# A scratch fill behind every second gather of adjacency rows

## The chip, the cores and the metric

The kernel runs on one core of a Trainium2 chip. The metric is the device time of one execution in microseconds, as the median of several runs. Beside the runs there is one execution taken by the hardware profiler; it is longer, and the lines of the profile belong to it alone.

The engines are named as in the profile: PE is TensorE (PEld its weight loads), DVE is VectorE, ACT is ScalarE, POOL is GpSimd, SP is SyncE. SP, ACT and POOL also issue the DMAs.

## The reference

Input are features `x` (2708 x 512), a sparse non-negative adjacency matrix `adj` (2708 x 2708, about 0.3% of it filled, densest in the first rows and columns, its diagonal filled) and small weights. Four graph layers follow one another, each with a residual and a layer norm:

```python
x = ln(x + L0(x, adj)); x = ln(x + L1(x, adj)); x = ln(x + L2(x, adj, adj)); x = ln(x + L3(x, adj))
L0: A = adj + I; d = 1/sqrt(rowsum(A)); (d[:,None] * A * d[None,:]) @ x @ W.T + b
L1: inc = adj + mask/norm(mask); (inc @ x) / rowsum(inc)        # mask = adj > 0
L2: sigmoid(gate_a * (softmax-like attention over the mask of adj) @ h + gate_b * (adj @ (x @ Wg) + bg))
L3: relu(adj @ (bin(x) @ sign(weight).T))
```

Every layer multiplies `adj` with rows of features. What the kernel saves is the zeros of `adj`.

## The kernel before, in words

The rows are cut into 22 blocks of 128 (the last has 20 rows). For each output block `b` the kernel doesn't multiply with all 22 column tiles of `adj`. It packs: it looks up which nodes are neighbours of any row of the block, lists them 128 at a time (`ROOM[b]` lists for block `b`, 9 for block 1 down to 1 for block 21), and gathers for each list two things: the rows of `adj_t` for these nodes, only the 128 columns of block `b` (tile `packed[b]`, written once and used by all layers), and in each layer the feature rows of these nodes (`gathered`, L582). A matmul of the two then stands for a whole column of tiles. Block 0 is dense and stays so; some blocks take a few tiles directly (`DIRECT`).

**The search** (L669 to L1264) makes the lists and the packed tiles, and prepares layer 0 beside it. The blocks arrive in the order 1, 2, ... 21, 0, one per turn (`turn`, L1180). A turn loads two half rows of `adj` for a later block through SP's queue (`load`, four half-row buffers), sums them on ACT (L765), marks the non-zeros on DVE (L828) and counts them on PE (L849); it also transposes and projects `x` (L1030, L1045), scales the product by the inverse root of the degree and stores it with a DMA from ACT's queue into `y_rows` in device memory (L1055). The blocks are searched in nine groups:

```python
GROUPS = ((1,), (2, 3), (4, 5), (6, 7, 8), (9, 10, 11), (12, 13, 14), (15, 16, 17), (18, 19, 20), (21,))
```

A few turns after the last block of a group has arrived, `list_nodes` (L966) computes on DVE the group's lists, `index_of` (L987) and `row_at` (L993), and appends one entry per list to `to_fetch`. At the end of each turn `fetch` (L1011) issues an indirect DMA from POOL for each entry: the adjacency gather of 128 rows of 128 fp32 (L1013). For the first six groups (`RESTED`) it issues behind each gather a fill of a scratch tile of 128 x 384 fp32 with zeros on POOL (L1018). Nothing reads the scratch tile. There are 107 adjacency gathers in all: 9, 15, 13, 17, 15, 13, 12, 12 and 1 by group, so 82 of them are followed by a fill.

[...] the search is written out by hand and held in that order (`in_order`, L591). POOL's queue in and behind the search is thus: set-up, the 107 adjacency gathers with the 82 fills, then the gathers of layer 0 from `y_rows`, and so on through the layers. Each gather carries one of eight completion semaphores in turn, and waits until the gather eight before it has landed. The first gather of a group waits for that group's `row_at`.

**Layer 0** (L1399) goes through the blocks in the order 0, 1, 21, 2, 3, ...: it gathers feature rows from `y_rows` (L584, ten buffers), multiplies them with the packed tiles (L1316), adds and normalises on DVE (L1424, L654), and stores the block into `x1_rows` (L1428). Layers 1 and 2 do the same from `x1_rows` and `x2_rows`, layer 3 from `xw_rows`. Between the blocks of layer 0 stand other steps, which also read the packed tiles (`count_positive`, L1103).

Of the kernel before, what the change touches and what calls it, by code (L numbers as in the profile page):

```python
# [495 lines left out]
def sparse_layers(ctx, tc, x, adj, adj_t, w0_t, b0, w_sa, a_sa, w_gcnb, b_gcnb, wa, ba, wb, bb, w3_t,  # L496
# [22 lines left out]
    def direct(b: int):  # L519

        return tuple(range(NB)) if b == 0 else DIRECT.get(b, ())
# [147 lines left out]
    with tc.tile_pool(name="s_pre", bufs=1) as pre:  # L669
# [134 lines left out]
        group_of = {b: g for g in GROUPS for b in g}  # L804
# [201 lines left out]

        to_fetch = []
        RESTED = GROUPS[:-3]
        rest = pre.tile([P, 384], F32, name="s_rest")

        def fetch(n: int):  # L1011
            for b, t, row in to_fetch[:n]:
                nc.gpsimd.indirect_dma_start(  # L1013
                    out=packed[b][:, t + len(direct(b)), :], out_offset=None, in_=adj_t,
                    in_offset=bass.IndirectOffsetOnAxis(ap=row, axis=0), element_offset=b * P,
                )
                if group_of[b] in RESTED:
                    nc.gpsimd.memset(rest, 0.0)  # L1018
            del to_fetch[:n]

# [159 lines left out]
        def turn(at: int):  # L1180
# [46 lines left out]
            if found_in == SOON:  # L1227
                list_nodes(SOON)
            fetch(len(to_fetch))
            if at == NTURN:  # L1230
                count_block0()
# [824 lines left out]
def kernel(  # L2056
# [25 lines left out]
    flag = ctx.enter_context(tc.tile_pool(name="flag", bufs=1))  # L2082
    over = flag.tile([1, 1], I32, name="over")
    sparse_layers(tc, *args, over)
    n_over = nc.values_load(over[0:1, 0:1], min_val=0, max_val=-(-x.shape[0] // P))
    with tc.If(n_over > 0):
# [43 lines left out]
```

## Time and profile before

| | before |
|---|---|
| median of 3 runs | 1017.79 us (1017.23 to 1019.32) |
| profiled execution | 1063.61 us |
| its span, first to last instruction | 1061.9 us |
| mean granted clock of PE | 0.942 |
| busy in the span: PE, DVE, ACT, POOL | 893.4, 663.5, 385.5, 569.7 us |
| adjacency gathers, L1013 | 107, 115.8 us, first start 24.9, last start 208.8 us |
| scratch fills, L1018 | 82, 44.0 us, first start 26.5, last start 175.9 us |
| gathers from `y_rows`, L584 | 107, first start 210.0, last start 365.9 us |

Times in views of the profile count from the start of the span. A group of instructions is named by its line, engine, operation and tile; a wait names the instruction that waited and what released it. The busy time of a DMA on POOL is the time in which POOL issues it, not the transfer. "Remote" or "an unknown queue" as a releaser means that the profile does not show what ended the wait. A line number of the changed kernel is two higher behind the change (L1013 becomes L1014, L1018 becomes L1020).

### The profile page before, as it was taken

The page shows a single profiled execution, that of the slowest core. Times are in us where ns is not written, and L with a number is a line of the kernel's source. Part 1 is how long each engine was busy: PE and PEld are TensorE (multiplying, and loading weights), DVE is VectorE, ACT ScalarE, POOL GpSimd, SP SyncE. Part 2 cuts the span into 40 slices and gives each one's busy share as a digit, 9 for nine tenths or more (in the row PEclk, how much of TensorE's full clock was granted, in tenths as well). Part 3 has the DMA queues.
Part 4 walks back from the last instruction along what each step waited for, and adds up shares of the span by engine and source line. Part 5 has one row for each costly group of instructions (what it writes and reads, how often), then busy time and mean ns, then how long its engine had stood idle before and what let it go on. Part 6 is the DMA issues. An engine that isn't in the chain of part 4 may idle for free.

```text
span 1061.9 us, 13166 instructions
## 1 busy us (share of the span) xinstructions
PE 893.4 (84%) x3793; PEld 465.5 (44%) x3793; DVE 663.5 (62%) x2571; ACT 385.5 (36%) x821; POOL 569.7 (54%) x621
## 2 busy tenths in 40 slices
PE   1989996078788978899999999998889999689994
PEld 1545552022123324455455543443535555467772
DVE  4899998125566745345555346666758877646666
ACT  3566662000000013445344334333334333255554
POOL 1799998766666544555434034534434333057762
PEclk9899999589898988999999999999999999989996
DMA  9999984356776745666645266668677665299986
GB/s 265 349 321 322 336 263 144 82 171 209 231 210 207 227 139 145 184 209 189 208 144 168 95 233 216 238 223 288 205 230 230 200 195 201 80 269 311 321 233 214
DMA packets 96294, 231.16 MB, mean 218 GB/s; under 512 B 14204, under 2 KB 27884, under 8 KB 96212
## 3 DMA queue, kind: packets, MB, share of 16 engines
q0 software_dynamic: 46896, 139.22, 44.3%
q1 hardware_dynamic: 37368, 76.25, 20.9%
q10 hardware_dynamic: 11948, 14.76, 4.3%
q8 instruction: 32, 0.52, 0.2%
q14 instruction: 50, 0.41, 0.1%
HBM read 188.51 MB, written 31.71 MB: 207 GB/s over the span
## 4 chain that ended last, share of the span: by engine, by line
PE 52%; DVE 12%; DMA 11%; POOL 10%; another core or an unknown queue 6%; issue 6%; ACT 3%; ACTq 0%; POOLq 0%; SPq 0%; DVEq 0%
PE l L1316 14%; DMA xg<-x_rows,i 8%; PE h L1533 7%; POOL a L1013 6%; PE l L1999 4%; PE a L1744 4%; PE e L1744 4%; PE l L2038 3%; POOL s_rest L1018 3%; PE pg L1796 2%; PE pc L1796 2%; PE l L1371 2%; PE e L1566 1%; PE px L1857 1%
## 5 line engine op out<-in xcount | busy, mean ns | idle before, releaser
L1721 POOL DMA_INDIRECT xg<-x_rows,i x107 | 106.2, 993 | 170.3 <-PE a L1744 40.9
L584 POOL DMA_INDIRECT xg<-x_rows,i x107 | 103.6, 968 | 115.9 <-PE l L1316 73.1
L1013 POOL DMA_INDIRECT a<-in_adj_t_dram,row_at x107 | 115.8, 1082 | 46.6 <-DVE deg L773 21.4
L584 POOL DMA_INDIRECT xg<-y_rows,i x107 | 104.6, 978 | 52.6 <-issue 24.1
L1316 PE MATMUL l<-xg,a 128*64 128x512 f32 (+1 forms) x214 | 98.0, 652 | 27.5 <-DMA xg<-y_rows,i 26.9
L584 POOL DMA_INDIRECT xg<-xw_rows,i x76 | 79.6, 1048 | 38.6 <-issue 17.9
L1744 PE MATMUL a<-xg,a 128*64 128x512 f32 (+1 forms) x214 | 92.8, 603 | 4.5 <-DMA xg<-x_rows,i 4.5
L1744 PE MATMUL e<-xg,ae 128*64 128x512 f32 (+1 forms) x214 | 90.3, 603 | 2.7 <-ACT ae L1494 2.6
L1533 PE MATMUL h<-s_wsa,xt 128*128 128x256 f32 (+3 forms) x352 | 83.8, 392 | 6.9 <-ACT xt L1528 6.8
L1045 PE MATMUL y<-s_w,xt 128*128 128x512 f32 (+1 forms) x176 | 86.9, 640 | 0.0
L1316 PE MATMUL l<-xg,inc 128*64 128x512 f32 (+1 forms) x214 | 79.4, 613 | 3.6 <-DMA xg<-x_rows,i 3.1
L1533 PEld LDWEIGHTS h<-s_wsa,xt 128*128 128x128 f32 (+1 forms) x352 | 65.0, 189 | 33.5 <-ACT xt L1528 15.6
L1489 ACT ACTIVATE ae<-sl,xg 128x64 f32<-128x64 f32 (+1 forms) x107 | 37.5, 359 | 99.1 <-DMA xg<-x_rows,i 88.6
L765 ACT ACTIVATE unused<-arow 128x1408 uint8<-128x1408 f32 (+3 forms) x44 | 58.3, 1325 | 3.8 <-DMA x_rows<-s_zero 3.0
L1316 PEld LDWEIGHTS l<-xg,a 128*64 128x64 f32 (+1 forms) x214 | 25.1, 160 | 78.4 <-DMA xg<-y_rows,i 41.5
L1424 DVE SCALAR_TENSOR_TENSOR t<-l,s_dinv,f 128x512 f32<-128x512 f32 (+1 forms) x21 | 15.6, 744 | 64.6 <-remote 44.7
L1999 PE MATMUL l<-ws,pw 128*128 128x512 f32 (+1 forms) x210 | 51.5, 400 | 3.9 <-DVE pw L1927 3.9
L613 ACT ACTIVATE rsqs<-mv 128x1 f32<-128x1 f32 (+2 forms) x56 | 11.3, 202 | 112.1 <-DVE mv L642 45.8
L1540 DVE COPY h<-h 128x260 f32<-128x260 f32 (+1 forms) x20 | 8.6, 428 | 66.3 <-PE h L1533 47.5
L1045 PEld LDWEIGHTS y<-s_w,xt 128*128 128x128 f32 (+1 forms) x176 | 33.8, 203 | 36.5 <-issue 36.4
L1490 DVE SCALAR_TENSOR_TENSOR ae<-ae 128x128 f32<-128x128 f32 (+5 forms) x56 | 19.2, 343 | 45.8 <-ACT ae L1489 45.1
L1796 PE MATMUL pg<-s_wg,pt 128*128 128x256 f32 (+1 forms) x176 | 44.7, 392 | 2.8 <-ACT pt L1784 2.8
(302 smaller groups left out, 1887.2 us busy)
## 6 DMA issues: line engine op xcount, KB each, us to landing
arow<-in_adj_dram SPq DMA_DIRECT2D x21, 704.0 KB
arow<-in_adj_dram SPq DMA_DIRECT2D x21, 650.0 KB
x_rows<-f SPq DMA_DIRECT2D x41, 256.0 KB
aw<-in_adj_t_dram SPq DMA_DIRECT2D x21, 320.0 KB
f<-in_x_dram SPq DMA_DIRECT2D x20, 256.0 KB
y_rows<-yt ACTq DMA_DIRECT2D x20, 256.0 KB
out_dram<-f SPq DMA_DIRECT2D x20, 256.0 KB
x_rows<-h SPq DMA_DIRECT2D x19, 257.0 KB
```

What stands on the lines that cost most here:

```text
L584: nc.gpsimd.indirect_dma_start(out=t, out_offset=None, in_=src[:, :], in_offset=bass.IndirectOffsetOnAxis(ap=index[b][:, i : i + 1], axis=0),)
L765: nc.scalar.activation(unused[:m, : ar.shape[1]], ar, AF.Copy, accum_out=row_sums[:m, b, h : h + 1])
L1013: nc.gpsimd.indirect_dma_start(out=packed[b][:, t + len(direct(b)), :], out_offset=None, in_=adj_t, in_offset=bass.IndirectOffsetOnAxis(ap ...
L1018: nc.gpsimd.memset(rest, 0.0)
L1045: nc.tensor.matmul(ps[:m], xt[:, k, :m], w0[:, k, :], start=(k == 0), stop=(k == KC - 1))
L1316: nc.tensor.matmul(ps[r0:r1], weights, moving, start=(i == order[0]), stop=all(span(b, j) != (r0, r1) for j in order[order.index(i) + 1 :] ...
L1489: nc.scalar.activation(ev[:, i, :], sl, AF.Identity, bias=score)
L1533: nc.tensor.matmul(ps, xt[:, k, :m], w[:, k, :], start=(k == 0), stop=(k == KC - 1))
L1721: nc.gpsimd.indirect_dma_start(out=g, out_offset=None, in_=x2_rows[:, :], in_offset=bass.IndirectOffsetOnAxis(ap=index[b][:, t : t + 1], a ...
L1744: nc.tensor.matmul(ps[r0:r1], weights, moving, start=(i == order[0]), stop=all(span(b, k) != (r0, r1) for k in order[order.index(i) + 1 :] ...
L1796: nc.tensor.matmul(ps, pt[:, k, :m], w[:, k, :], start=(k == 0), stop=(k == KC - 1))
L1999: nc.tensor.matmul(whole[b], p[:r, h, b * P : (b + 1) * P], g[:r, :], start=(j == 0 and h == 0), stop=(j == NB - 1 and h == 1),)
```

## The change

The fill stands behind every second gather instead of behind each one. The counter counts all adjacency gathers, in the order in which they are issued; the fill follows the even ones of the first six groups.

```diff
         to_fetch = []
         RESTED = GROUPS[:-3]
+        fetched = [0]
         rest = pre.tile([P, 384], F32, name="s_rest")
 
         def fetch(n: int):
             for b, t, row in to_fetch[:n]:
                 nc.gpsimd.indirect_dma_start(
                     out=packed[b][:, t + len(direct(b)), :], out_offset=None, in_=adj_t,
                     in_offset=bass.IndirectOffsetOnAxis(ap=row, axis=0), element_offset=b * P,
                 )
-                if group_of[b] in RESTED:
+                fetched[0] += 1
+                if group_of[b] in RESTED and fetched[0] % 2 == 0:
                     nc.gpsimd.memset(rest, 0.0)
             del to_fetch[:n]
```

## The prediction

> **What bounds the kernel now.** I read the page first: its busy shares, its forty slices and its chain of waits. GpSimd (POOL) is busy in 54% of the span, TensorE (PE) in 84%, yet two POOL lines of the search stand in the chain.
>
> ```profile
> PE 52%; DVE 12%; DMA 11%; POOL 10%; another core or an unknown queue 6%; issue 6%; ACT 3%; ACTq 0%; POOLq 0%; SPq 0%; DVEq 0%
> PE l L1316 14%; DMA xg<-x_rows,i 8%; PE h L1533 7%; POOL a L1013 6%; PE l L1999 4%; PE a L1744 4%; PE e L1744 4%; PE l L2038 3%; POOL s_rest L1018 3%; PE pg L1796 2%; PE pc L1796 2%; PE l L1371 2%; PE e L1566 1%; PE px L1857 1%
> ```
>
> So the scratch fill itself (L1018) is 3% of the chain and the adjacency gathers (L1013) 6%. Next, the waits up to 270 us, and the busy time by stretch, to see who stands still while POOL works:
>
> ```profile
> DVE t L1424 <- remote: 41.5, 1, 41.5
> PE l L1316 <- DMA xg<-y_rows,i: 26.9, 5, 24.9
> ...
> 178.00:210.00 32.00, 2.92 (x14) 0.84 (x13) 10.27 (x36) 0.41 (x2) 24.65 (x24) 0.54 0.48 132
> ```
>
> The columns of the last line are the stretch, its length, and busy us of PE, PE's weight loads, DVE, ACT and POOL, then clock, DMA share and GB/s. From 178 to 210 us PE works 2.9 us, ACT 0.4, POOL 24.7 of 32: TensorE waits 24.9 us in one piece for the first gathered row tile of layer 0 (`xg<-y_rows`). Why is that gather late? The POOL timeline at three places (start, length, what, and after it the idle time before it):
>
> ```profile
> 144.47 1.00 POOL L1013 DMA_INDIRECT a<-in_adj_t_dram,row_at  x1 [0.16 <-issue]
> 145.47 0.47 POOL L1018 MEMSET s_rest<- 128x384 f32 x1
> 146.10 1.16 POOL L1013 DMA_INDIRECT a<-in_adj_t_dram,row_at  x1 [0.16 <-issue]
> 147.26 1.07 POOL L1018 MEMSET s_rest<- 128x384 f32 x1
> 148.49 1.34 POOL L1013 DMA_INDIRECT a<-in_adj_t_dram,row_at  x1 [0.16 <-issue]
> ...
> 207.51 0.94 POOL L1013 DMA_INDIRECT a<-in_adj_t_dram,row_at  x1 [0.30 <-issue]
> 208.76 0.94 POOL L1013 DMA_INDIRECT a<-in_adj_t_dram,row_at  x1 [0.30 <-issue]
> 210.01 0.94 POOL L584 DMA_INDIRECT xg<-y_rows,i  x1 [0.30 <-issue]
> ```
>
> From 45.57 to 226 us POOL has no pause longer than 0.31 us. Its queue holds 107 adjacency gathers, then the gathers of `y_rows`, in that order; the first of these starts at 210.01 because the last adjacency gather starts at 208.76. What it needs was there long before: the last store of `y_rows` is issued at 175.78, and SP's own read of `y_rows`, which waits for it, is issued at 177.97. So for 32 us only POOL's backlog holds layer 0 back. The search is not the limit there: its lists (`row_at` on DVE) start at 45.12, 69.30, 91.52, 111.52, 132.25, 151.97, 169.84 and 175.90, while POOL reaches the first gather of each of these groups at 45.57, 74.39, 98.27, 127.74, 155.56, 176.52, 193.78 and 208.76. Its lateness grows from 0.3 to 33 us.
>
> [...] the instruction takes 0.94 us, and by the packets the data land some 5 us after its start in the crowded search and 2.2 us near 205 us. [...] gathers of 0.94 us stretch to 1.4 to 1.6 while DVE is over 95% busy, and 13 of the 82 fills take about 1 us, not 0.44. [...]
>
> **The change, part by part.** On PE, DVE, ACT and SP the instructions and their order stay the same; only POOL's list changes. Of 82 fills (9+15+13+17+15+13 gathers of the first six groups) every odd one goes: 41.
>
> One removed fill: its own time, plus the 0.16 us that the next gather waits behind it, minus the 0.30 us between two gathers with nothing between (as from 178 us on). With the usual 0.44 us that is 0.44 + 0.16 − 0.30 = 0.30 us. With the mean over all fills (44.0 us / 82 = 0.537) it is 0.40.
>
> The first group's five (at 26.5, 30.2, 33.9, 37.1 and 40.2 us) are worth nothing: after its ninth gather POOL waits 4.9 us for the next list at 45.1, and only that wait grows. If that list came earlier, they would be worth another 1.5 us. There remain 36. Low end: 36 × 0.30 = 10.9 us. High end: the 36 that go took 19.6 us together, six of them long ones of about 1.04; 19.6 + 36 × (0.16 − 0.30) = 14.5 us. The 3.6 us between the ends [...] (6 × 0.6), which the next gather may inherit, since DVE is as busy as before. I take half of it: 12.7 us.
>
> Do lists then hold POOL up? By the third group POOL is 7 × 0.35 = 2.5 us ahead of before: 71.9, and the list is done at 70.0. By the fourth it is 14 × 0.35 = 4.9 ahead: 93.4 against 91.7. Behind that the gap widens: 118 against 112, 164 against 152. So no wait, by 1.7 us at the closest. Each gather also waits for the landing of the gather eight before it; eight new intervals are 8 × 1.6 = 13 us, against some 5 us to landing. No wait either.
>
> Gathers run earlier, beside the row loads. In 45.5 to 150 us the DMA engines are 94% busy at 315 GB/s. About six more gathers fall into it (57 with intervals of 1.86 us, 63 with 1.68). A gather costs 0.29 us of all sixteen engines (192 to 208 us: the software queue 25.4% of 16 us for 14 gathers). So 6 × 0.29 = 1.7 us later at most for the loads, hidden: between POOL's new first `y_rows` gather (210.0 − 12.7 = 197.3) and the ready `y_rows` (178) lie 19 us. If that cover went, the 1.7 us would count.
>
> From 197 us on everything stands in the same order behind POOL's gathers and PE's matmuls with them. DVE and ACT have finished their opening work of layer 0 at 190.2 us and wait for the first block, so nothing else is late next. In layer 0 POOL is busy 105 of 168 us and PE 136 by turns, each waiting for the other; both start 12.7 us earlier, and I carry it one to one through layers 1 to 3, which have no clock time of their own to wait for.
>
> Sum: span 1061.9 − 12.7 = 1049.2 us; the execution adds 1.7 around it (1063.6). The median of the runs, 1017.79, is 4.3% below the profiled execution, whose page cannot say where. POOL's chain leads by tens of us in the trace, so it should lead there too, and I take the same absolute gain: 1017.8 − 12.7 = 1005.1 us. Scaling it would change 0.5 us.
>
> **The rivals.**
>
> *Lists or loads eat part.* POOL speeds up, DVE's lists come a few us later by contention, and at the fourth group, whose margin is 1.7 us, POOL waits. For it: DVE is 99.3 of 104.5 us busy in the search, DMA 94%. Against it: that wait comes before 22 of the 36 fills that go, and these still gain afterwards: 22 × 0.35 = 7.7. Time about 1010 to 1014.
>
> *Nothing moves.* [...] a gather behind a gather stretches by what the fill took. For it: gathers of 1.4 to 1.6 us stand in the search only. Against it: the median gather there is 0.97, near the 0.94 without any DVE work, and most fills sit at 0.44[...]. Time 1017.8.
>
> *Slower: pairs of gathers hold DVE.* [...] `s_dia_pos` (L1095) takes 0.69 us at 114.30 and ends with POOL's gather; on one column it takes 0.13 at 159.07, so DVE pays for POOL. If each of 41 pairs cost DVE one gather more, 41 × 0.94 = 38 us, `y_rows` would be ready at 216 instead of 178, POOL's first gather of it would slip from 210 to 216: about 1024. It decides from 32/41 = 0.78 us per pair. Against it: POOL was never free before either (busy 95 of 104 us), and the share of time in which it executes falls[...].
>
> **How the numbers follow.** Gain as worked out 0.72, part of it 0.10, nothing 0.08, slower 0.10. Differences below about 0.2% (2 us) are what a measurement here cannot tell from no change: the three runs spread by 2.1 us. Faster 0.72 + 0.10 = 0.82, same 0.08, slower 0.10. The likeliest case alone: 1003.3 to 1006.9 by its two ends, 1001 to 1008 with the spread and with TensorE's clock, whose half-speed stretches may fall elsewhere. For eight in ten the second case comes in, and the edge of the third: 1001 to 1016.
>
> **What would show it.** Right: 41 fills of `s_rest`; first `y_rows` gather near 197; DVE's wait of 41.5 us at L1424 near 29; the last `row_at` still within 2 us of 175.9; gathers of the search at the same mean of about 1.1 us. Step wrong, lists: an idle POOL before L1014 for a DVE `row_at`. Step wrong, [...] longer gathers and a gain under 10 us at the first `y_rows` gather. Step wrong, carrying: that gather at 197 but the end not 12 us earlier. The whole is wrong if the search's last list moves beyond 195 us, because then DVE or the loads, not POOL's queue, set when layer 0 begins.

## The result, and the profile after

The changed kernel takes 1003.52 us (median of 6 runs, 1000.5 to 1007.23), the kernel before in the same comparison 1018.76 (6 runs, 1017.23 to 1022.14): a ratio of 0.9849, interval 0.9821 to 0.9876. That is 15.2 us less; 12.7 had been forecast, and 1003.52 lies inside the likeliest case's own range.

The kernel before itself took about 1017 us in some of the comparisons and about 1066 us in others (the 1017 level and the 1066 level below), so each comparison has its own runs of the kernel before beside it. The profile of before shown above (1063.61 us) is of the 1066 level, that of the changed kernel (1000.5 us) of the 1017 level. It was therefore not the profiler that made the profiled execution of before longer than its runs. To compare like with like there is a profile of the kernel before at the 1017 level as well (1022.25 us, span 1020.5; "the third run of before" below).

The page of the changed kernel, chain of waits:

```profile
PE 53%; DMA 20%; DVE 16%; issue 4%; ACT 3%; POOL 3%; ACTq 0%; POOLq 0%; DVEq 0%; SPq 0%
PE l L1318 11%; DMA xg<-x_rows,i 10%; PE h L1535 8%; DMA xg<-y_rows,i 7%; PE l L2001 5%; PE a L1746 4%; PE e L1746 4%; PE l L2040 3%; PE y L1047 3%; PE pg L1798 2%; DVE s_mask L828 2%; PE pc L1798 2%; PE e L1568 2%; PE a L1569 2%; POOL xg L584 1%
```

POOL's share of the chain is 3%; the scratch fill and the adjacency gather are no longer among the lines that the page names, and a line of the search on DVE (`s_mask`, L828) has come in. The same page of the third run of before:

```profile
PE 54%; DMA 19%; POOL 12%; DVE 8%; issue 4%; ACT 2%; ACTq 0%; POOLq 0%; SPq 0%
```

Here POOL has 12%. This shift alone shows little: in the first comparison below another profile of the kernel before has POOL at 2% and DVE at 15%, and POOL's queue still ends 27 us behind the last list in the changed kernel (194.44 and 167.48). The queue itself is the better witness. Next the waits up to 270 us and the stretch from 178 to 210 us (columns as in the prediction) of the changed kernel:

```profile
DVE t L1426 <- PE l L1318: 41.1, 7, 29.2
PE l L1318 <- DMA xg<-y_rows,i: 24.8, 12, 18.9
...
178.00:210.00 32.00, 12.80 (x29) 3.53 (x29) 4.06 (x20) 0.00 (x0) 24.38 (x26) 0.60 0.50 131
```

PE does 12.8 us of work in the stretch in which it did 2.9; its longest wait for the first gathered tile is 18.9 us instead of 24.9 (23.4 in the third run of before). POOL's timeline:

```profile
97.58 0.95 POOL L1014 DMA_INDIRECT a<-in_adj_t_dram,row_at  x1 [0.30 <-issue]
98.52 0.44 POOL L1020 MEMSET s_rest<- 128x384 f32 x1
99.12 1.56 POOL L1014 DMA_INDIRECT a<-in_adj_t_dram,row_at  x1 [0.16 <-issue]
100.98 0.99 POOL L1014 DMA_INDIRECT a<-in_adj_t_dram,row_at  x1 [0.30 <-issue]
...
162.10 0.44 POOL L1020 MEMSET s_rest<- 128x384 f32 x1
...
194.44 0.95 POOL L1014 DMA_INDIRECT a<-in_adj_t_dram,row_at  x1 [0.30 <-issue]
195.70 0.95 POOL L584 DMA_INDIRECT xg<-y_rows,i  x1 [0.30 <-issue]
```

Two gathers, one fill, with the 0.30 and 0.16 us between them that the forecast used; the first gather of `y_rows` at 195.70 (forecast 197.3). In the third run of before the queue ends so:

```profile
208.42 0.95 POOL L1013 DMA_INDIRECT a<-in_adj_t_dram,row_at  x1 [0.30 <-issue]
209.67 0.95 POOL L584 DMA_INDIRECT xg<-y_rows,i  x1 [0.31 <-issue]
```

Like for like, then, that gather moves by 209.67 − 195.70 = 14.0 us, and the median by 15.2.

### The profile page after: what moved, and what is told of

It is laid out like the page before. It is cut to its first block, busy times and chain, and to the rows that moved or that the text cites. A ratio compares the mean times of both kernels' runs of the same rounds, so it can differ in the third digit from the quotient of the medians.

```text
span 998.8 us, 13107 instructions
## 1 busy us (share of the span) xinstructions
PE 875.6 (88%) x3775; PEld 458.8 (46%) x3793; DVE 657.8 (66%) x2571; ACT 386.5 (39%) x821; POOL 549.6 (55%) x580
## 4 chain that ended last, share of the span: by engine, by line
PE 53%; DMA 20%; DVE 16%; issue 4%; ACT 3%; POOL 3%; ACTq 0%; POOLq 0%; DVEq 0%; SPq 0%
PE l L1318 11%; DMA xg<-x_rows,i 10%; PE h L1535 8%; DMA xg<-y_rows,i 7%; PE l L2001 5%; PE a L1746 4%; PE e L1746 4%; PE l L2040 3%; PE y L1047 3%; PE pg L1798 2%; DVE s_mask L828 2%; PE pc L1798 2%; PE e L1568 2%; PE a L1569 2%; POOL xg L584 1%
## 5 line engine op out<-in xcount | busy, mean ns | idle before, releaser
L1014 POOL DMA_INDIRECT a<-in_adj_t_dram,row_at x107 | 115.9, 1083 | 52.2 <-issue 24.9
L1047 PE MATMUL y<-s_w,xt 128*128 128x512 f32 (+1 forms) x176 | 83.6, 620 | 0.0
L638 DVE BATCH_NORM_STATS2 st<-t 128x6 f32<-128x512 f32 (+1 forms) x66 | 45.2, 685 | 0.2
```

The lines of the kernel that those rows point to most:

```text
L638: nc.vector.bn_stats(st[:m], t[:m])
L1014: nc.gpsimd.indirect_dma_start(out=packed[b][:, t + len(direct(b)), :], out_offset=None, in_=adj_t, in_offset=bass.IndirectOffsetOnAxis(ap ...
L1047: nc.tensor.matmul(ps[:m], xt[:, k, :m], w0[:, k, :], start=(k == 0), stop=(k == KC - 1))
```

## The experiments

Nothing reads the scratch tile, so every kernel here computes all that the reference does; only POOL's time and its place differ. All edits are given against the kernel before or against the changed one, as named.

The theory (the backlog): POOL's queue is the gate to layer 0, and the time is set by how much work stands in it ahead of the first `y_rows` gather, not by where fills stand. The rival (crowding): gathers close behind each other cost something elsewhere, so fewer fills lose again what they save.

### First: no fills, the same fills in pairs, the saved time put back at the end

The kernel before again:

> The kernel before, unchanged, profiled once more. In its first profile the last list (row_at) started at 175.9 us, in the changed kernel at 167.5. If fewer fills make DVE's search faster, it is again near 176 here. If the first profile was merely a slow execution (clock 0.942, 1063.6 us), it is near 168, the span near 1017, and the first gather from y_rows still near 207 to 210, since POOL's own instructions set that.

1068.61 us, ratio 1.0002 (0.9978 to 1.0026). This comparison fell on the 1066 level. The last list starts at 178.31 us and the first `y_rows` gather at 209.29, so the list is near 176 again and not near 168.

No fills at all:

```diff
-        RESTED = GROUPS[:-3]
+        RESTED = ()
```

> All 82 fills are gone. POOL's queue as the limit: 41 more fills of about 0.35 us leave, so the first gather from y_rows comes up to 14 us before 195.7, until POOL catches up with the lists; the last two groups still have 13 gathers of 1.25 us behind the list of 161 us, so not before 178: 178 to 185 us, and the kernel takes about 988 to 994 us. Lists as the limit: POOL idles before gathers of the fourth group onward and the gain is under 8 us. Pairs holding DVE: the lists come later than in the changed kernel by 5 us or more and the time is no better than 1003.

1102.33 us, ratio 1.0308 (1.0235 to 1.0380): slower. First `y_rows` gather at 239.6, against 209.3 in the kernel before beside it. So at this level crowding is real. The waits from 45 to 180 us say where it bites:

```profile
POOL a L1014 <- DVE s_own L1064: 42.9, 4, 14.1
ACT xt L1039 <- remote: 39.1, 4, 12.1
DVE s_dia_own L858 <- remote: 27.7, 4, 9.5
```

POOL now waits for lists, 42.9 us in four pieces, and DVE and ACT stand still for up to 12 us with no releaser shown. One of those stalls in the timeline of the same kernel:

```profile
86.32 0.64 PE L1032 MATMUL pt<-s_ident,f 128*128 128x128 f32 x4
...
92.17 0.94 POOL L1014 DMA_INDIRECT a<-in_adj_t_dram,row_at  x1 [0.30 <-issue]
93.42 0.94 POOL L1014 DMA_INDIRECT a<-in_adj_t_dram,row_at  x1 [0.30 <-issue]
96.48 0.16 DVE L858 SCALAR_TENSOR_TENSOR s_dia_own<-find,s_dia 128x1 f32<-128x1 f32 x1 [9.51 <-remote]
96.53 0.59 ACT L1039 COPY xt<-pt 128x512 f32<-128x512 f32 x1 [10.08 <-remote]
```

ACT's copy takes the four transposes that the record has ended at 86.96, but starts at 96.53; DVE resumes with it, about 3 us after the start of the last gather of the burst. That gather ends at 94.36 and POOL is idle from there to the end of the stall. No view prints it, but the trace also keeps when each semaphore was updated. DVE and ACT both wait here for the semaphore that PE updates, and its two updates stand at 96.45 and 96.51 us, 10.0 and 9.6 us after the end of the matmuls that send them (86.46 and 86.96). So the signal of PE came late; DVE and ACT took it within 0.03 us. By stretch (columns as in the prediction):

```profile
84.00:92.00 8.00, 6.76 (x44) 3.68 (x43) 2.90 (x14) 2.42 (x4) 6.04 (x7) 1.00 0.80 260
92.00:96.40 4.40, 0.00 (x0) 0.00 (x0) 0.00 (x0) 0.00 (x0) 1.89 (x2) 0.79 0.39 113
96.40:98.50 2.10, 0.85 (x13) 0.57 (x12) 1.73 (x9) 1.56 (x4) 0.00 (x0) 0.50 0.00 0
98.50:112.00 13.50, 11.47 (x87) 6.42 (x85) 10.88 (x47) 7.39 (x13) 2.96 (x3) 0.64 0.85 287
```

In 4.4 us nothing works but POOL's last two gathers, and PE's clock is at half after it: PE's last matmul before the stall ends at 91.25, and the granted clock is at 0.50 from 94.55 to 108.20. So to the 4.4 us without work comes a stretch of 13.65 us at half clock that began in the stall. What lowered the clock, and why PE's signal comes so late, the trace does not show.

Two fills behind every second gather, so that gathers stand in pairs but no fill is saved (against the changed kernel):

```diff
                 if group_of[b] in RESTED and fetched[0] % 2 == 0:
                     nc.gpsimd.memset(rest, 0.0)
+                    nc.gpsimd.memset(rest, 0.0)
```

> The gathers stay in pairs as in the changed kernel, but two fills stand behind each pair, so there are 82 again. POOL's queue as the limit: POOL's time is that of the kernel before within 2 us, first gather from y_rows at 207 to 211, and the kernel takes 1014 to 1020 us, as before. Pairing itself as the cause of the gain [...]: it stays near 1003.

1078.11 us, ratio 1.0113 (1.0050 to 1.0176); first `y_rows` gather 217.5, 8.2 us later than before. POOL's timeline:

```profile
123.98 0.95 POOL L1014 DMA_INDIRECT a<-in_adj_t_dram,row_at  x1 [0.15 <-issue]
125.24 0.94 POOL L1014 DMA_INDIRECT a<-in_adj_t_dram,row_at  x1 [0.31 <-issue]
126.18 0.44 POOL L1020 MEMSET s_rest<- 128x384 f32 x1
126.67 0.42 POOL L1021 MEMSET s_rest<- 128x384 f32 x1
127.25 1.05 POOL L1014 DMA_INDIRECT a<-in_adj_t_dram,row_at  x1 [0.16 <-issue]
```

A pair takes 3.27 us; two gathers each with its fill take 2 × (0.94 + 0.44 + 0.16) = 3.08. The 0.19 us are 0.30 instead of 0.16 between the gathers and 0.05 between the fills; for the 36.5 pairs from the second group on, 7 of the 8.2 us. The rest is the second group's list, which came 1.5 us later (46.12, not 44.64). The last list, at 179.83, is within 2 us of the kernel before beside it (178.31). So with two fills behind each pair the search is hardly delayed even at this level, although ACT waits there five times for PE without a seen releaser (15.4 us, 4.2 at most): the loss is mostly POOL's queue.

The changed kernel, with 36 fills put between the last adjacency gather and the first `y_rows` gather:

```diff
                 if group_of[b] in RESTED and fetched[0] % 2 == 0:
                     nc.gpsimd.memset(rest, 0.0)
+                if b == NB - 1:
+                    for _ in range(36):
+                        nc.gpsimd.memset(rest, 0.0)
```

> The changed kernel with 36 fills put back in one place, between the last adjacency gather and the first gather from y_rows. POOL's queue as the limit: 36 x 0.44 = 16 us later at that gather, at about 211, and the kernel takes 1003.5 + 16 = about 1019 us. If the gain came from the search (faster lists, DVE or loads freed from the fills), the search is as in the changed kernel, and the time stays under 1008.

1085.38 us, ratio 1.0183 (1.0118 to 1.0247); `y_rows` at 231.7. Its last adjacency gather starts at 212.0, 4 us later than in the kernel before beside it (208.0), although 41 fewer fills stand ahead of it. So at this level the search ate the saving. Whether the changed kernel alone still gains there was not in this comparison; it came in the last one.

### Second: the changed kernel again, the saving without pairs, a part of the change

This comparison fell on the 1017 level. The changed kernel:

> The changed kernel, unchanged, once more. Queue theory (POOL's queue alone decides, gathers in a row cost nothing): 0.982 to 0.988 of the kernel before wherever it runs, first gather from y_rows 13 to 15 us before that of the kernel before. Crowding theory (gathers in a row hold up TensorE's handing on of results while the search loads): where the kernel before takes about 1068 us, the search shows waits of ACT and DVE for TensorE that end with no seen releaser, the last list comes 5 us or more later than before, and the ratio is 0.995 or more; where it takes about 1018, none of this and 0.985.

1004.13 us against 1017.01, ratio 0.9863 (0.9807 to 0.9920); `y_rows` at 197.4.

A fill behind each gather, as before, but of half the width:

```diff
                 if group_of[b] in RESTED:
-                    nc.gpsimd.memset(rest, 0.0)
+                    nc.gpsimd.memset(rest[:, :192], 0.0)
```

> A fill behind every gather, as in the kernel before, but of 192 columns instead of 384. By the lengths of fills of 1, 128 and 384 columns (0.10, 0.20, 0.44 us) a fill of 192 takes 0.26 us, so POOL saves 0.175 us on each of 73 fills that count: 12.8 us, as much as the change. Queue theory: the same ratio as the changed kernel within 0.004. Crowding theory, where the kernel before takes about 1068 us: no two gathers stand in a row, so better than the changed kernel by 0.005 or more.

Ratio 0.9876 (0.9821 to 0.9932), median 1007.79; `y_rows` at 197.1. The median fill takes 0.278 us, 0.16 less than 0.44: over the 73 fills from the second group on 11.7 us, about as much as the change saves, and POOL starts on the second group 1.4 us earlier. The gain and the place of the first `y_rows` gather are those of the change, within the intervals. What counts at this level is POOL's time, not whether gathers stand in pairs.

All fills of the sixth group taken out, the others as before:

```diff
-        RESTED = GROUPS[:-3]
+        RESTED = GROUPS[:-4]
```

> The kernel before without the 13 fills of the sixth rested group alone (blocks 12 to 14), whose gathers ran from 155.6 to 175.9 us, when the row loads of the search had ended. Both theories: 13 x 0.30 to 0.40 = 4 to 5 us less, ratio 0.995 to 0.996, with the first gather from y_rows that much earlier and no new waits, since nothing is left to be crowded.

1013.24 us, ratio 0.9958 (0.9939 to 0.9978): 4.3 us of 1017.01. `y_rows` at 205.6, 4.0 us earlier than in the third run of before. Thirteen fills × 0.35 = 4.6. The last list, at 174.05, moved by only 1.7 us, and the queue ends 30 us behind it, so a faster search is not where this gain comes from.

The kernel before, for its profile at this level:

> The kernel before, unchanged, as the profile to compare these three with: first gather from y_rows at 207 to 210 us and the last list at 175 to 179 where it takes about 1068 us; where it takes about 1018, by the queue theory the same gather near 209, and the last list near 168.

1022.25 us in this one run; first `y_rows` gather at 209.67. No wait with an unknown releaser stands in its search, nor in that of the changed kernel at this level.

### Third: no fills at the 1017 level

> All 82 fills gone, once more. If the loss of 3% seen where the kernel before took 1068 us is a matter of gathers in a row and nothing else, it is slower here too, wherever it runs, with waits for TensorE without a seen releaser in the search. If it needs the conditions of those runs, then, with the kernel before at about 1017 us, the queue theory holds to the end: first gather from y_rows at 178 to 187 us and about 0.970 to 0.978 of the kernel before.

> The changed kernel on the same chip as the run without fills. With the kernel before at about 1017 us: 0.984 to 0.988 again. With it at about 1068 us: crowding theory 0.995 or more, queue theory 0.982 to 0.988.

Without any fill (the edit of the first comparison): 991.95 us against 1017.60, ratio 0.9736 (0.9698 to 0.9774). The changed kernel in the same comparison: 1002.21, 0.9857 (0.9799 to 0.9914). The end of POOL's search queue without fills:

```profile
182.51 0.95 POOL L1014 DMA_INDIRECT a<-in_adj_t_dram,row_at  x1 [0.30 <-issue]
183.77 0.94 POOL L584 DMA_INDIRECT xg<-y_rows,i  x1 [0.30 <-issue]
```

The other half of the fills is worth another 12 us (195.70 to 183.77), and none of the stalls of the first comparison appears: the waits from 45 to 180 us show no unknown releaser, and DVE is busy 96.3 us of the 104.5 from 45.5 to 150, where the same kernel at the 1066 level had 63.4. At the 1017 level this kernel beats both others; at the 1066 level it loses 3.1%.

### Fourth: the saved time put back, beside the changed kernel

> The changed kernel with 36 fills put back in one place, between the last adjacency gather and the first gather from y_rows, once more. With the kernel before at about 1017 us, queue theory: the adjacency gathers as in the changed kernel (last start 194 to 196 us), the first gather from y_rows 16 us later than there, at 211 to 214, and the gain gone: 1016 to 1022 us, ratio 0.998 to 1.004. If the gain came from the faster search or from anything but POOL's queue: ratio 0.99 or less. With the kernel before at about 1068 us: 1.018 as seen there.

> The changed kernel beside it. With the kernel before at about 1017 us: 0.984 to 0.988 again, last adjacency gather at 194 to 196. With it at about 1068 us: crowding theory 0.995 or more, queue theory 0.982 to 0.988.

It fell on the 1066 level again (before 1065.20). Fills at the end: 1081.30 us, ratio 1.0161 (1.0091 to 1.0231). The changed kernel: 1064.37, 0.9971 (0.9948 to 0.9995). The two differ only in the 36 fills:

```profile
209.33 1.06 POOL L1014 DMA_INDIRECT a<-in_adj_t_dram,row_at  x1 [0.31 <-DVE pos L1108]
210.39 18.01 POOL L1023 MEMSET s_rest<- 128x384 f32 x36
229.05 0.95 POOL L584 DMA_INDIRECT xg<-y_rows,i  x1 [0.65 <-issue]
```

Their searches end alike (last adjacency gather at 209.33 and 209.79), the first `y_rows` gather at 229.05 and 211.04: 18.0 us apart. The medians are 16.9 us apart (20.2 by the two ratios). Work of POOL at that place passes to the end nearly one to one, at this level too.

The changed kernel's own saving is lost there in the search. DVE and POOL in its timeline:

```profile
187.29 0.16 DVE L912 COPY base<-find 128x3 f32<-128x3 f32 x1 [9.09 <-remote]
...
194.03 0.17 DVE L993 TENSOR_SCALAR row_at<-i 128x12 int32<-128x12 int32 x1 [0.22 <-DVE i L987]
...
194.47 0.94 POOL L1014 DMA_INDIRECT a<-in_adj_t_dram,row_at  x1 [8.76 <-DVE s_own L1064]
```

After a run of gathers with no fills between them (the seventh group, which has none in the kernel before either; the last starts at 184.77) DVE has stood for 9.1 us, the list comes at 194.03, and POOL has waited 8.8 us for it; the last list comes at 201.30. PE's signal that ends DVE's wait is 8.8 us late. This is the rival in which lists hold POOL up. The profile of before could not show it, although it belongs to this level: with a fill behind each gather its search ran as at the 1017 level.

### All of them together

`y_rows` is the start of the first such gather; each is read from one profile, and its shift is against the kernel before at the same level (209.67 at 1017, 209.3 at 1066); the shift of the time is (ratio − 1) × the median of the kernel before beside it.

| kernel | level | `y_rows` at | shift | ratio | shift of the time |
|---|---|---|---|---|---|
| the change | 1017 | 195.7, 197.4, 195.8 | −14.0, −12.3, −13.8 | 0.9849, 0.9863, 0.9857 | −15.4, −13.9, −14.6 |
| half fills | 1017 | 197.1 | −12.6 | 0.9876 | −12.6 |
| five groups | 1017 | 205.6 | −4.0 | 0.9958 | −4.3 |
| no fills | 1017 | 183.8 | −25.9 | 0.9736 | −26.9 |
| the change | 1066 | 211.0 | +1.7 | 0.9971 | −3.1 |
| two per pair | 1066 | 217.5 | +8.2 | 1.0113 | +12.1 |
| fills at end | 1066 | 231.7, 229.1 | +22.4, +19.8 | 1.0183, 1.0161 | +19.6, +17.1 |
| no fills | 1066 | 239.6 | +30.3 | 1.0308 | +32.9 |

The start of the first `y_rows` gather tells the time to within 5 us in every row and at both levels. In one row, the change at the 1066 level, the two have opposite signs: the gather came 1.7 us later and the time fell by 3.1, and no run shows where that was gained. The backlog theory is right about the gate. The crowding rival is right about what can fill the way to it, at one of the two levels.

## Why the prediction was right, and where it was not

**The gate.** POOL's queue was said to hold layer 0 back. Right: every variant moves the time by what it moves the first `y_rows` gather, within 5 us. That it could be read from a profile of the 1066 level was luck: the first 210 us of before are alike at both levels, and the change is worth little at the level that was profiled.

**The size of a fill.** 12.7 us for the 36 fills, the middle between 10.9 (36 × 0.30 is 10.8) and 14.5. From the first gather of the second group to the first of `y_rows` the third run of before takes 209.67 − 46.39 = 163.28 us, the changed kernel 195.70 − 44.58 = 151.12: 12.2 us (11.1 and 12.0 in its other two profiles at this level). Right within 2 us, and the value between the two ends was the better one. The gathers got longer, as the forecast had allowed for: their mean is 1.083 us, near the 1.1 that was forecast, and 1.051 in the third run of before.

**The first group's five are worth nothing, unless its next list came earlier.** The condition came true: the second list stands at 44.14 instead of 45.94, and POOL starts on it 1.8 us earlier (44.58 and 46.39), where the forecast had allowed for up to 1.5. With it 12.2 + 1.8 = 14.0, the whole shift of the gather. That the removed fills did this is not shown: with five groups, where the first group has all its fills, that list stands at 43.77.

**Lists do not hold POOL up.** Right at the 1017 level: behind the first list, the wait of 5.4 us for the second group's (6.8 in the other two profiles) is POOL's only one for lists in the search. At the 1066 level wrong, as shown.

**Carried one to one.** Right: −14.0, −12.3 and −13.8 us at the gather, −15.4, −13.9 and −14.6 in the time. The 0.8 to 1.6 us by which the time gains more lie inside the intervals.

**The last list stays within 2 us of 175.9.** This step failed. It came at 167.48, and at 167.02 and 165.76 in the other two profiles at this level, against 175.76 in the third run of before. The last list of that run and of the changed kernel:

```profile
175.76 0.15 DVE L993 TENSOR_SCALAR row_at<-i 128x1 int32<-128x1 int32 x1 [0.15 <-DVE root_h L624]
167.48 0.15 DVE L993 TENSOR_SCALAR row_at<-i 128x1 int32<-128x1 int32 x1 [0.16 <-DVE root_h L624]
```

The reasoning had the change leave DVE's pace alone ("since DVE is as busy as before"). DVE is as busy, but gets further: its instructions became shorter. The groups of DVE from 45.5 to 178 us (line, shape, count, then busy us and mean ns), third run of before:

```profile
L828 DVE TENSOR_SCALAR s_mask<-arow 128x1408 bf16<-128x1408 f32 (+3 forms) x34 | 35.0, 1031 | 0.0
L943 DVE TENSOR_SCALAR after<-s_slot,base 128x384 bf16<-128x384 int16 (+4 forms) x54 | 17.8, 455 | 0.0
L1066 DVE SCALAR_TENSOR_TENSOR f<-yt,s_own,f 128x512 f32<-128x512 f32 (+1 forms) x20 | 15.1, 755 | 0.9 <-DVE s_own L1062 0.2
```

And the changed kernel:

```profile
L828 DVE TENSOR_SCALAR s_mask<-arow 128x1300 bf16<-128x1300 f32 (+3 forms) x33 | 31.2, 945 | 0.0
L1068 DVE SCALAR_TENSOR_TENSOR f<-yt,s_own,f 128x512 f32<-128x512 f32 (+1 forms) x20 | 15.1, 755 | 0.8 <-DVE s_own L1064 0.2
L943 DVE TENSOR_SCALAR after<-s_slot,base 128x384 bf16<-128x384 int16 (+4 forms) x54 | 14.3, 369 | 0.0
```

Both instructions with one tensor as input got 86 ns shorter in the mean: 33 × 0.086 + 54 × 0.086 = 7.5 of the 8.3 us by which the last list moved. It is not the mix of shapes: the mean of `s_mask` with 128 x 1408 goes from 1094 to 1032 ns, with 128 x 1300 from 963 to 875, that of `after` with 128 x 384 from 494 to 382. The one with two tensors is unchanged at 755 ns. Half fills give 924 and 341 ns and the last list at 166.05, no fills 874 and 313 ns and 165.18; the one with two tensors takes 753 and 756 ns in these. What makes those two shorter and not this one is not shown. The forecast had priced only the other direction, POOL's gathers of 1.4 to 1.6 us beside a busy DVE, and had what POOL costs DVE only as a danger. At the 1017 level the faster search cost and gained nothing behind POOL's queue, unless the 1.8 us at the second group come from it.

**DVE's wait of 41.5 us near 29.** It reads 29.2, and that is chance (31.8 in each of the other two profiles at this level). In the third run of before the wait is 35.04 us:

```profile
225.50 0.75 DVE L1424 SCALAR_TENSOR_TENSOR t<-l,s_dinv,f 128x512 f32<-128x512 f32 x1 [35.04 <-PE l L1316]
```

In the changed kernel it ends at 211.27 after 29.21 us. It ends 14.2 us earlier, but also begins 8.4 us earlier, at 182.06 instead of 190.46, because the search was done earlier. The 41.5 of the profile that the forecast used holds 6 us more, up to 231.67, of the 1066 level; the signal of PE that ends it is itself over 4 us late. Two errors of the step, 6 us and 8 us, cancel.

**Slower by pairs of gathers.** This rival had the right place and the wrong mechanism. It put the loss on DVE waiting out one gather more, 0.94 us a pair, and had it decide from 0.78. No run shows that: pairs without any saving left the last list within 2 us of where it was, and at the 1017 level DVE's instructions were shorter with no fills at all. What was seen at the 1066 level is DVE and ACT waiting for late signals of PE, up to 12 us at a time, once gathers follow without fills. There the change is worth 0.3%, not 1.5%. The prediction was made for 1017.79 us and tested there.

**Left open.** What sets the level. The third and the fourth comparison ran on the same chip ten minutes apart and fell on different levels, so it is not the chip alone. The traces show what differs: 826 instructions of PE update its semaphore. In the seven profiles at the 1017 level 823 to 826 of these updates are recorded, and none comes more than 0.1 us after the end of its instruction (the last two of each program left out). In the seven at the 1066 level 674 to 700 are recorded, and 51 to 86 of them come more than 1 us late, up to 11.8. In the two profiles of the kernel before at that level only one such update each lies ahead of 210 us, in the changed kernel 23, with two fills per pair 12 (none over 2 us), with no fills 19. So at that level a fill behind every gather went with a search nearly free of late signals, and what the kernel before loses there it loses in the layers: "another core or an unknown queue" takes 6 and 7% of its chain, and does not appear in it at the 1017 level. Why PE's signals come late, and why they do so in the search once gathers follow without fills, stays open: nothing was tried that separates the transfers from their issue, such as the same gathers of fewer bytes. Putting the 36 fills back at the end was seen only at the 1066 level.

## What to carry to other kernels

Where a queue runs late without a pause, as POOL's did here, an instruction in it that nobody reads costs its net interval (here 12.2 / 36 = 0.34 us: its duration plus the gap behind it, less the gap that stands there without it), and the arrival of the next stage's first instruction tells most of the gain. Before pricing a removal on POOL, look at what DVE's instructions do beside it: here two kinds with one tensor as input got 86 ns shorter in the mean. And a pacing instruction can be dead weight in one condition and protection in another, so compare its removal more than once, and against the kernel before each time: taking all fills out gave −2.6% here and +3.1% there.

## What the runs showed of the hardware that was not expected

- One program, two levels: the kernel before at 1017.0 to 1018.8 us in three comparisons and 1065.2 and 1068.5 in two, with a mean granted clock of PE of 0.956 in the profile at the one level and of 0.942 and 0.932 in the two at the other. The first 210 us are alike (209.67 and 209.3 at the first `y_rows` gather); the 45.5 us between the spans (1066.0 and 1020.5) come later.
- At the lower level PE's semaphore follows the end of its instruction within 0.1 us; at the upper level, in every kernel, 51 to 86 of its recorded updates come more than 1 us late.
- At the upper level, without fills, DVE and ACT waited up to 9.5 and 12.1 us for signals of PE whose instructions had ended, and PE's clock was at 0.50 after one of these waits, until 108.20 us; DVE's busy time from 45.5 to 150 us fell from 97.1 to 63.4 us of 104.5. At the lower level the same program had 96.3.
- With fewer fills on POOL (128 x 384 fp32, 0.44 us each) two kinds of one-tensor instruction on DVE were shorter at the lower level: with 82 fills their means were 1031 and 455 ns, with 41 they were 945 and 369, with none 874 and 313.
